# The first two outer sets of a masked-linear and gated-FFN kernel: multiplying x before or after its norm

## The chip, the cores and the metric

The kernel runs on one core of one Trainium2 chip. The metric is the device time of the core in microseconds (us): 513.37 is the median of three runs of the kernel before (513.25 to 513.42). TensorE multiplies; VectorE, ScalarE and GpSimd do elementwise work; SyncE's queue (SP) issues nearly all transfers between device memory and the on-chip memory. TensorE writes into eight accumulator banks, which VectorE and ScalarE can read[...].

## The reference, cut to what matters

x has 2048 rows (tokens) of 512 elements.

```python
xn  = (x - mean(x)) / sqrt(var(x) + eps)                 # per row
s   = xn @ (weight * block_mask).T                       # 512 x 512
nx  = xn * rsqrt(mean(xn * xn) + eps) * ln_w
h   = silu(nx @ gate_w.T) * (nx @ up_w.T)                # 1792 wide each
out = x + s * silu(h @ down_w.T)
```

## The kernel before, in words

**Layout.** Everything is kept transposed: features lie on the 128 partitions, tokens along the free axis, in tiles of 128 x 512 float32. The 2048 tokens are four tiles t; x^T has four feature chunks c. The norm and the RMS norm are joined in two factors per token, `scl` and `nb` (minus the mean times `scl`); a normalised x is `scl * x + nb`. `ln_w` is multiplied into the gate and up weights (`scaled`, `scale_a`).

**Products.** Each matrix product is done as Strassen-Winograd's seven products in place of eight, in two levels: an outer level over quarters of the matrices, and within it an inner level over quarters of these. The gate and up weights come as seven groups of 256 rows (g = 0 to 6), the masked weight is an eighth. For each group the outer level has seven sets q = 1 to 7. One set is one `instance`: seven products m = 1 to 7 of a 128 x 128 weight tile with a 128 x 512 tile of x^T. They are summed in accumulator banks named x, y and z with the set's number j: `x_2` is the bank x of set j = 2. An instance ends with four result tiles. Sets q = 1 and 2 of all groups come first (j = 0 to 15; q = 1 and 2 of group 0 are j = 0 and 1), because they use only the plain quarters; the results of q = 2 are q = 1's plus its own products (the `prior` of `instance`). Then come q = 6, 5, 7, 3 and 4, and last the down projection.

**Sums around the products.** The products m = 5, 6, 7 and 4 need differences of x^T tiles (`inner_b`, on VectorE and GpSimd), and m = 3, 5, 6 and 7 need sums of weight tiles (`inner_a`, four of them for q = 1 and 2 of a group, s1, s2, s4 and s3, on GpSimd). Between the products a bank is copied ("snap") or added to others ("seed", "total"), on ScalarE where there is no prior and on VectorE where there is.

**The start.** Sixteen 128-row blocks of x are loaded (`load_x`), each tile's statistics are taken on VectorE (`stats`), the factors are worked out (`factors`, with a square root on ScalarE), the blocks are scaled and shifted (`normalise`), transposed by TensorE into a bank (`transpose`) and copied out by ScalarE (`evacuate`). Only tiles 0 and 1 are needed by sets q = 1 and 2. Until the first transposes, TensorE does products of the identity with itself (`warm`).

**The order of the work.** It is written out by hand. `at(pos, fn)` files every step under a position, and at the end all steps are issued in the order of their positions. One position is the time of one product, and set j begins at 7j; `EARLY` and the positions T(us) set the start apart. So the order within each engine's queue is fixed. What must wait for what is settled by semaphores that the framework adds. Buffers are fixed slots of one array `mem` (rings with names such as B5, B7, acc), and banks rotate under four names (X 3, Y 2, Z 1, V 2). The transposes of tile 3, about positions 51 to 59, go into the V banks, as does `gate`, the result of the SiLU.

**After a set.** When group g's sets q = 1 and 2 are complete, `silu` (ScalarE) and `h_out` (VectorE's product of the gate, L414 before, L487 after) make the quarter of h from its four tiles, a column n at a time: n = 0 and n = 1. Set q = 1's four results go to `acc_dram[g]` and come back later for q = 6.

Of the kernel before, what the change touches and what calls it, by code (L numbers as in the profile page):

```python
# [8 lines left out]
F32 = mybir.dt.float32  # L9
# [22 lines left out]
def tile_masked_linear_gated_ffn(  # L32
# [19 lines left out]
    h_dram = tc.dram_tile([7, G, 2, P, W], F32, name="h_dram")  # L52
    s_dram = tc.dram_tile([KC, NTT, P, W], F32, name="s_dram")
    rms_dram = tc.dram_tile([NT], F32, name="rms_dram")
    acc_dram = tc.dram_tile([G + 1, P, 4, W], F32, name="acc_dram")
    dw_dram = tc.dram_tile([4, P, G, 256], F32, name="dw_dram")

# [25 lines left out]
    def slot(tag, name=None):  # L83
        i, n = ring[tag]
        ring[tag][0] += 1
        return mem[:, first_slot[tag] + i % n, :]
# [6 lines left out]
    def bank(tag, name):  # L93
        return ps.tile([P, W], F32, tag=tag, name=name, bufs=PSB[tag])
# [8 lines left out]
    ident = const.tile([P, P], F32, tag="ident", name="ident")  # L103
    blockones = const.tile([P, P], F32, tag="blockones", name="blockones")
    keep = const.tile([P, 4, 16], F32, tag="keep", name="keep")

    def constants():
        make_identity(nc, ident)
        nc.gpsimd.memset(blockones, 0.0)
        for b in range(P // BLK):  # L110
            nc.gpsimd.memset(blockones[b * BLK : (b + 1) * BLK, b * BLK : (b + 1) * BLK], 1.0)


    xt, raw, stat = {}, {}, {}
    agg = small.tile([P, NTT, TT, 2], F32, tag="agg", name="agg", bufs=1)
    rms = small.tile([P, NTT, TT], F32, tag="rms", name="rms", bufs=1)

    def load_x(t):
        for i in range(TT):
            xt[t, i] = mem[:, first_slot[("B6", "vc", "v5", "B4")[t]] + i, :]  # L120
            nc.sync.dma_start(xt[t, i], x[(t * TT + i) * P : (t * TT + i + 1) * P, :])

    def stats(t, i):
# [4 lines left out]
    def factors(t):  # L128


        scl = small.tile([P, TT], F32, tag="scl", name=f"scl_{t}")
        nb = small.tile([P, TT], F32, tag="nb", name=f"nb_{t}")
        stat[t] = (scl, nb)

        def last():
            nc.vector.reciprocal(scl, scl)
            nc.vector.scalar_tensor_tensor(nb, agg[:, t, :, 0], -1.0, scl, ALU.mult, ALU.mult)

        return [lambda: nc.vector.tensor_scalar(scl, agg[:, t, :, 1], 1.0 + EPS, EPS * EPS, ALU.mult, ALU.add),
                lambda: nc.scalar.activation(scl, scl, AF.Sqrt), last]  # L140

    def normalise(t, i, eng, cols=slice(0, W)):
        scl, nb = stat[t]
        v = xt[t, i][:, cols]
        if eng is dve:
            nc.vector.tensor_scalar(v, v, scl[:, i : i + 1], nb[:, i : i + 1], ALU.mult, ALU.add)
            return
        nc.scalar.activation(v, v, AF.Identity, bias=nb[:, i : i + 1], scale=scl[:, i : i + 1])

# [162 lines left out]
    def inner_a(g, part, k0=0, n=2):  # L312
# [8 lines left out]
        for k in range(n):  # L321
# [2 lines left out]
        return [lambda: add(pool, s1, a21, a22), lambda: add(pool, s2, s1, a11, ALU.subtract),  # L324
                lambda: add(pool, s4, a12, s2, ALU.subtract), lambda: add(pool, s3, a11, a21, ALU.subtract)]

    def weights(g, q, m):
        if q < 3 and m in (1, 2, 4):
            return aq[g, 0, q - 1][:, {1: 0, 2: 2, 4: 3}[m] * P :][:, :P]
        return aop[g, q][m]  # L330


    def instance(j, g, q, prior, dest, after):
# [1 line left out]

        st = {}

        seeded = j > 1

        def mm(m, tag, key, first):  # L340
            if first and key not in st:
                st[key] = bank("Y" if key == "z" and j == 1 else tag, f"{key}_{j}")
            nc.tensor.matmul(st[key], weights(g, q, m), operand(q, m), start=first and not (key == "z" and seeded),  # L343
                             stop=True, skip_group_check=True)

        def seed():

            if seeded:
                st["z"] = bank("Z", f"z_{j}")
                nc.scalar.copy(st["z"], st["x"])  # L350
            else:
                st["s1"] = slot("s2" if j else "s5", f"s1_{j}")
                if prior is None:
                    nc.scalar.copy(st["s1"], st["x"])
                else:
                    add(dve, st["s1"], st["x"], prior(0))
# [15 lines left out]
            else:  # L372
                add(dve, dest(i), st[key], prior(i))

        at(EARLY.get((j, 0), 7 * j + 1), seed)
        for off, m, tag, first, snapshot, out in (
            (0, 1, "X", True, None, None),
            (2, 5, "Y", True, ("s5", 3), None),
            (3, 2, "Z", True, None, (None, 0)),
            (4, 6, "X", False, ("s2", 1), None),  # L380
            (6, 3, "Y", False, None, ("s2", 1)),
            (8, 7, "X", False, None, ("s5", 3)),
            (12, 4, "X", False, None, (None, 2)),
        ):
            key, pos = tag.lower(), 7 * j + off
            at(EARLY.get((j, m), pos), mm, m, tag, key, first)
            if snapshot:
                at(pos + 1, snap, key, *snapshot)
            elif out:

                pos += 2.3 if prior is None and m == 2 and seeded else 1
                if m == 2:
                    pos = EARLY.get((j, "z"), pos)
                at(pos, total, key, *out)
                after(out[1], pos)


    def group(g, where):
# [39 lines left out]
        def summed(dst, src, into, then=None, engines=(pool,) * 4):  # L438
# [14 lines left out]
            3: (vc, vc, done(0, 1, vc)),  # L453
            4: (acc, acc, done(1, 0, acc)),
        }
        for q in setup:
            instance(where[g, q], g, q, *setup[q])

        def h_sum(q, n, tile_of, a, b):

# [2 lines left out]
            nc.sync.dma_start(h_dram[HD[q], g, n], o)  # L463

        sums, rest = slots(F["acc"] + 4 * (g % 2), 4), 7 * where[g, BLOCKS[0]]
        at(7 * where[g, 1] + 15, lambda: nc.sync.dma_start(acc_dram[g], sums))
        at(rest - (14 if g else 6), lambda: nc.sync.dma_start(sums, acc_dram[g]))
        if g < G:
            def again():
# [114 lines left out]
    def down_instance(o, q, where_, prior, dest, after):  # L584
# [78 lines left out]
        if last_set:  # L663
            at(where_(17) + 0.1, base_of_last)
            for part, pos in zip(parts, (where_(23), where_(24), where_(25))):
# [8 lines left out]
    where = {gq: j for j, gq in enumerate(order)}  # L674
    N = len(order)
    END = 7 * N
    T = lambda us: (us - 14.0) / 0.86
    EARLY.update({(0, 1): T(10.4), (0, 2): T(11.3), (1, 1): T(12.1), (1, 2): T(13.0), (0, 0): T(11.5), (1, 0): 4.3,
                  (0, "z"): 3.26, (1, "z"): 4.9})
    SILU = 26.2  # L680
    at(T(-10), constants)
    at(T(-10), load_x, 0)
    at(T(-10), lambda: nc.scalar.dma_start(lnw_sb, ln_w))

    at(T(-10), lambda: nc.gpsimd.tensor_copy(mem[:, F["a1"], 0:1], xt[0, 0][:, 0:1]))
    for K in range(2):
        at(T(-10), load_a, 0, K)
    at(T(-10), load_x, 1)
    for K in range(2):
        at(T(-10), load_a, 1, K)  # L690
    at(T(-10), load_x, 2)
    for K in range(2):
        at(T(-10), load_a, 2, K)
# [7 lines left out]
        for _ in range(n):  # L701
            nc.tensor.matmul(b[:, :P], ident, ident, start=True, stop=True, skip_group_check=True)

    at(T(1.4), lambda: warm(26, bank("V", "idle")))
    for t, p, step in ((0, T(7.1), 0), (1, T(12.5), 0), (2, 36.0, 1.2), (3, 36.1, 1.2)):
        plan(p, step, factors(t))
    for i in range(TT):
        half = act if i < 2 else dve
        at(T(3.7 + 0.82 * i), stats, 0, i)
        at(T(9.35 + 0.82 * i), stats, 1, i)  # L710
        for h, cols in enumerate((slice(0, W // 2), slice(W // 2, W))):
            at(T(7.95 + 0.9 * h + 0.4 * (i % 2)), normalise, 0, i, half, cols)
            at(T(13.45 + 0.9 * h + 0.4 * (i % 2)), normalise, 1, i, half, cols)
        for c in range(KC):
            at(T((8.9, 9.3, 9.8, 11.0)[c] + 0.05 * i), transpose, 0, c, (2, 3, 0, 1)[i], "XYYX"[c])
            at(T((14.35, 14.8, 15.25, 16.2)[c] + 0.05 * i), transpose, 1, c, (2, 3, 0, 1)[i], "XVVV"[c])
    at(T(6.0), scale_a, 0, 0, pool)
    at(T(6.1), scale_a, 0, 1, pool)
    for c in range(KC):
        at(T((9.75, 10.3, 10.85, 12.05)[c]), evacuate, 0, c, act)  # L720
        at((5.6, T(15.6), 6.0, 3.14)[c], evacuate, 1, c, act)
    for pos, q, m, eng in ((1.1, 1, 5, dve), (1.87, 1, 6, dve), (2.56, 1, 7, dve), (3.95, 2, 5, dve), (2.7, 1, 4, pool),
                           (4.6, 2, 6, dve), (7.2, 2, 7, dve), (5.0, 2, 4, pool)):
        at(pos, inner_b, q, m, eng)
    for q in (1, 2):
        for k in (0, 1):
            for n in (0, 1):
                at(8, outer_b, q, k, n, None)
    at(2.1, scale_a, 1, 0)
    at(5.2, scale_a, 1, 1)  # L730
    for i in range(TT):
        at(14.0 + 2.5 * i, stats, 2, i)
        at(25.0 + 3 * i, stats, 3, i)
        at((44.0, 51.0, 55.2, 58.2)[i], normalise, 2, i, act)
        at(40.5 + 2.4 * i, normalise, 3, i, dve)
    plan(36.2, 1.2, rms_factor())

    for t, p0 in ((3, 51.5), (2, 65.5)):
        n = t % 2
# [21 lines left out]
    for g in range(G + 1):  # L761
        p, rest = 7 * where[g, 1], 7 * where[g, BLOCKS[0]]
        for K in range(2):
# [3 lines left out]
                at(p - (10.4, 7.3)[K], lambda K=K: mask_a(aq[G, 0, K], 0, K))  # L767
            elif g > 1:
                at(p - (10.4, 7.3)[K], scale_a, g, K)
        if g:  # L770
            plan(p - 7, 1, inner_a(g, 1))
        else:
            plan(T(9.9), 0, inner_a(0, 1, 0, 1))
            plan(T(11.9), 0, inner_a(0, 1, 1, 1))
        at(rest - 29, load_block, g)

        def block_sums(g=g):
# [147 lines left out]
```

## Time and profile before

| | |
|---|---|
| median of three runs | 513.37 us |
| the profiled execution | 513.17 us |
| its span, from the first to the last instruction | 511.4 us |
| TensorE (PE) busy | 505.8 us, 99% |
| VectorE (DVE) busy | 380.4 us, 74% |
| GpSimd (POOL) busy | 340.9 us, 67% |
| ScalarE (ACT) busy | 182.6 us, 36% |
| transfers | 121.59 MB, mean 238 GB/s |

The busy shares are means over the whole span. "L702" is line 702 of the kernel that was run, and a line can be a helper's: L97 is every elementwise add. PEld is TensorE's loading of weights. A float32 product shows as two MATMUL records and two LDWEIGHTS records, a transpose as one of each. The span's parts are given in us from its start. In a table by windows the columns are the length, then for PE, PEld, DVE, ACT and POOL the busy us with the number of instructions, then the granted TensorE clock, the share of the transfer engines and GB/s. In a timeline they are the start, the time and the instruction, and in brackets how long the engine stood idle before it and what released it. A row by form has busy us and the mean ns of one, then the idle time before.

### The profile page before, as it was taken

The page shows a single profiled execution, that of the slowest core. Times are in us where ns is not written, and L with a number is a line of the kernel's source. Part 1 is how long each engine was busy: PE and PEld are TensorE (multiplying, and loading weights), DVE is VectorE, ACT ScalarE, POOL GpSimd, SP SyncE. Part 2 cuts the span into 40 slices and gives each one's busy share as a digit, 9 for nine tenths or more (in the row PEclk, how much of TensorE's full clock was granted, in tenths as well). Part 3 has the DMA queues.
Part 4 walks back from the last instruction along what each step waited for, and adds up shares of the span by engine and source line. Part 5 has one row for each costly group of instructions (what it writes and reads, how often), then busy time and mean ns, then how long its engine had stood idle before and what let it go on. Part 6 is the DMA issues. An engine that isn't in the chain of part 4 may idle for free. (4 is left out here: it accounts for less than half of the span.)

```text
span 511.4 us, 4943 instructions
## 1 busy us (share of the span) xinstructions
PE 505.8 (99%) x1269; PEld 231.8 (45%) x1269; DVE 380.4 (74%) x590; ACT 182.6 (36%) x348; POOL 340.9 (67%) x283
## 2 busy tenths in 40 slices
PE   8999999999999999999999999999999999999997
PEld 8444444444444444444444444444444444444444
DVE  6878689876977969699696978968747645367736
ACT  4656754633536353353634433330100101001111
POOL 5522224994795968869597789976662754739960
PEclk9999999999999999999999999999999999999999
DMA  8436636369159386785948667499997698476472
GB/s 289 164 132 238 247 133 227 135 236 350 48 219 348 147 302 228 238 289 208 338 166 294 209 239 254 169 332 383 357 339 270 204 374 327 146 252 216 151 229 83
DMA packets 60460, 121.59 MB, mean 238 GB/s; under 512 B 5760, under 2 KB 13328, under 8 KB 58384
## 3 DMA queue, kind: packets, MB, share of 16 engines
q1 hardware_dynamic: 60288, 121.27, 66.8%
q8 instruction: 10, 0.16, 0.1%
q14 instruction: 18, 0.15, 0.1%
q10 hardware_dynamic: 144, 0.00, 0.0%
HBM read 75.11 MB, written 46.15 MB: 237 GB/s over the span
## 5 line engine op out<-in xcount | busy, mean ns | idle before, releaser
L97 POOL TENSOR_TENSOR mem<-mem 128x512 f32<-128x512 f32 (+4 forms) x245 | 305.2, 1267 | 135.4 <-ACT mem L264 36.5
L343 PE MATMUL x<-mem 128*128 128x512 f32 x448 | 213.6, 595 | 0.2 <-DVE mem L97 0.2
L343 PEld LDWEIGHTS x<-mem 128*128 128x128 f32 x448 | 83.7, 190 | 107.3 <-issue 86.9
L97 DVE TENSOR_TENSOR mem<-x,mem 128x512 f32<-128x512 f32 x137 | 92.5, 684 | 42.0 <-PE x L343 41.1
L343 PE MATMUL y<-mem 128*128 128x512 f32 x224 | 114.5, 593 | 0.3 <-DVE mem L97 0.3
L97 DVE TENSOR_TENSOR mem<-mem 128x512 f32<-128x512 f32 (+3 forms) x60 | 74.7, 1252 | 7.8 <-PE dx L591 4.3
L591 PE MATMUL dx<-mem 128*128 128x512 f32 x174 | 78.3, 592 | 0.0
L97 DVE TENSOR_TENSOR mem<-y,mem 128x512 f32<-128x512 f32 x96 | 65.6, 684 | 9.8 <-PE y L343 8.5
L343 PEld LDWEIGHTS y<-mem 128*128 128x128 f32 x224 | 42.2, 190 | 53.0 <-issue 47.8
L350 ACT COPY z<-x 128x512 f32<-128x512 f32 x54 | 30.9, 573 | 97.9 <-PE x L343 92.2
L343 PE MATMUL z<-mem 128*128 128x512 f32 x112 | 57.3, 593 | 0.0
L591 PEld LDWEIGHTS dx<-mem 128*128 128x128 f32 x174 | 33.1, 190 | 41.6 <-issue 40.4
L591 PE MATMUL dy<-mem 128*128 128x512 f32 x98 | 44.5, 592 | 0.0
L409 ACT ACTIVATE gate<-mem 128x512 f32<-128x512 f32 x56 | 33.1, 601 | 25.3 <-DVE mem L97 20.9
L414 DVE TENSOR_TENSOR mem<-gate,mem 128x512 f32<-128x512 f32 x56 | 38.0, 681 | 5.1 <-POOL mem L97 4.3
L564 POOL TENSOR_TENSOR mem<-mem 128x512 f32<-128x512 f32 x16 | 25.0, 1570 | 15.3 <-DMA mem<-s_dram 15.2
L343 PEld LDWEIGHTS z<-mem 128*128 128x128 f32 x112 | 21.0, 190 | 24.9 <-issue 23.9
L574 ACT ACTIVATE silu<-mem 128x512 f32<-128x512 f32 x15 | 9.0, 602 | 64.6 <-DVE mem L97 48.3
L97 DVE TENSOR_TENSOR mem<-z,mem 128x512 f32<-128x512 f32 x41 | 28.0, 682 | 3.5 <-PE z L343 3.5
L591 PEld LDWEIGHTS dy<-mem 128*128 128x128 f32 x98 | 18.6, 190 | 23.4 <-issue 23.4
L97 DVE TENSOR_TENSOR mem<-dx,mem 128x512 f32<-128x512 f32 x16 | 11.0, 690 | 20.1 <-PE dx L591 20.1
L591 PE MATMUL dz<-mem 128*128 128x512 f32 x56 | 25.2, 592 | 0.0
(73 smaller groups left out, 289.2 us busy)
## 6 DMA issues: line engine op xcount, KB each, us to landing
h_dram<-mem SPq DMA_DIRECT2D x98, 256.0 KB, 2.1
mem<-h_dram SPq DMA_DIRECT2D x28, 768.0 KB, 6.2
mem<-in_gu SPq DMA_DIRECT2D x42, 256.0 KB, 3.7
acc_dram<-mem SPq DMA_DIRECT2D x8, 1024.0 KB, 4.2
mem<-acc_dram SPq DMA_DIRECT2D x8, 1024.0 KB, 6.7
mem<-in_x SPq DMA_DIRECT2D x16, 256.0 KB, 5.2
s_dram<-mem SPq DMA_DIRECT2D x16, 256.0 KB, 4.8
mem<-s_dram SPq DMA_DIRECT2D x16, 256.0 KB, 6.3
```

The source lines that it names most:

```text
L97: eng.tensor_tensor(o, a, b, op)
L343: nc.tensor.matmul(st[key], weights(g, q, m), operand(q, m), start=first and not (key == "z" and seeded), stop=True, skip_group_check=True)
L350: nc.scalar.copy(st["z"], st["x"])
L409: nc.scalar.activation(gate[key], t(), AF.Silu)
L414: nc.vector.tensor_mul(a(), gate[key], b())
L564: at_later.append(lambda: nc.gpsimd.tensor_tensor(s_tile, s_tile, rms_bc[t], ALU.mult))
L574: nc.scalar.activation(b[0][:, part], y[:, part] if source is None else source(), AF.Silu)
L591: nc.tensor.matmul(st[key], w(), b(), start=first and key != "z", stop=True, skip_group_check=True)
```

## The change

Sets j = 0 and 1 (group 0, q = 1 and 2) no longer use the normalised and transposed x. The kernel loads the eight tiles of x^T that they need straight from an input that holds x transposed (`raw_x`), takes the differences from them (`raw_t`) and multiplies these. The norm is made good afterwards: for a weight row w, w (scl x + nb) is scl (w x) + nb sum(w).

- The row sums of group 0's weights are TensorE products with a column of ones (`sum_rows`, eight products of one column).
- The factors `scl` and `nb` of tiles 0 and 1 lie token by token on the partitions. They are transposed by TensorE, copied by ScalarE, stored in device memory and read back as four tiles with the same row on all partitions (`fac_store`).
- Each of the eight results is multiplied by the row of `scl` on GpSimd and a shift is added there; the shift is ScalarE's product of the row of `nb` with the row sum. Then q = 1's and q = 2's tiles are added (`raw_results`): for each of the four tile places i, five GpSimd operations. The two sets have no prior any more, and their results lie in other slots. `acc_dram[0]` is stored at position 49.
- Normalising, transposing and evacuating tiles 0 and 1 move behind the products of j = 0 and 1, for use from j = 2 on, and parts of the normalising go to GpSimd. The scaling of group 0's first weights moves from GpSimd to ScalarE, that of group 1's from ScalarE to GpSimd.
- The loads' order changes: group 0's weights and the eight x^T tiles come ahead of x. The one-column GpSimd copy that kept the weights behind the first block of x is gone. The idle products are 8 and no longer 26.
- `EARLY` and the positions of the start are written anew, with 9.9 in the place of 14.0 in T.

The diff, cut to its core:

```diff
+    def raw_x(q, k, n, eng=nc.sync):
+        o = rop[q, k, n] = mem[:, RQ[q - 1][2 * k + n], :]
+        c = 2 * (q - 1) + k
+        eng.dma_start(o, x_t[c * P : (c + 1) * P, n * W : (n + 1) * W])
...
+    def sum_rows(rs, K):
+        for r in range(2):
+            for c in range(2):
+                nc.tensor.matmul(rs[:, 2 * K + r : 2 * K + r + 1], aq[0, 0, K][:, (2 * c + r) * P :][:, :P], ones,
+                                 start=c == 0, stop=c == 1, skip_group_check=True)
+
+    def fac_store():
+        b = bank("V", "fac_rows")
+        nc.tensor.transpose(b[: 4 * TT, :P], fac.rearrange("p a t i -> p (a t i)"), ident)
+        rows = small.tile([4 * TT, P], F32, tag="fac_rows", name="fac_rows", bufs=1)
+        nc.scalar.copy(rows, b[: 4 * TT, :P])
+        nc.sync.dma_start(fac_dram.rearrange("a t (i p) -> (a t i) p", p=P), rows)
+        for a in range(2):
+            for t in range(2):
+                nc.sync.dma_start(fac_bc(a, t), fac_dram[a, t].unsqueeze(0).to_broadcast([P, W]))
...
+    def raw_results(p1, c11, silu, h_out):
+
+        tmp = [mem[:, F["B7"] + k, :] for k in range(7)] + [mem[:, F["B5"] + 1, :]]
+
+        def shift(K, i):
+            r, n = divmod(i, 2)
+            nc.scalar.mul(tmp[4 * K + i], fac_bc(1, n), row_sums[:, K, r : r + 1])
+
+        pos = 22.0
+        for n in (0, 1):
+            for i in (n, n + 2):
+                at(pos - 0.1, shift, 0, i)
+                at(pos, lambda i=i, n=n: add(pool, p1(i), p1(i), fac_bc(0, n), ALU.mult))
+                at(pos + 1.5, lambda i=i: add(pool, p1(i), p1(i), tmp[i]))
+                at(pos + 2.9, shift, 1, i)
+                at(pos + 3, lambda i=i, n=n: add(pool, c11(i), c11(i), fac_bc(0, n), ALU.mult))
+                at(pos + 4.5, lambda i=i: add(pool, c11(i), c11(i), tmp[4 + i]))
+                at(pos + 6, lambda i=i: add(pool, c11(i), c11(i), p1(i)))
+                pos += 7.5
+            at(pos + 0.2, *silu(n))
+            at(pos + 1.5, *h_out(n))
...
-        at(7 * where[g, 1] + 15, lambda: nc.sync.dma_start(acc_dram[g], sums))
+        if g:
+            at(7 * where[g, 1] + 15, lambda: nc.sync.dma_start(acc_dram[g], sums))
+        else:
+            at(49, lambda: nc.sync.dma_start(acc_dram[0], slots(R1, 4)))
...
-    T = lambda us: (us - 14.0) / 0.86
+    T = lambda us: (us - 9.9) / 0.86
...
     at(T(-10), constants)
+    at(T(-10), load_a, 0, 0)
+    at(T(-10), lambda: nc.scalar.dma_start(lnw_sb, ln_w))
+    at(T(-10), raw_x, 1, 0, 0, nc.scalar)
...
-    at(T(-10), lambda: nc.gpsimd.tensor_copy(mem[:, F["a1"], 0:1], xt[0, 0][:, 0:1]))
...
-    at(T(1.4), lambda: warm(26, bank("V", "idle")))
+    at(T(1.4), lambda: warm(8, bank("V", "idle")))
+
+    at(T(4.0), scale_a, 0, 0)
+    at(T(6.3), scale_a, 0, 1)
...
+    at(T(17.0), row_sums_of, 0)
+    at(T(21.2), row_sums_of, 1)
+    at(T(22.4), fac_store)
```

## The prediction

> **What bounds the kernel now.** I read the page's busy shares first, then the windows of the stages, then the engines' timelines of the first 75 us. From the page:
>
> ```profile
> PE 505.8 (99%) x1269; PEld 231.8 (45%) x1269; DVE 380.4 (74%) x590; ACT 182.6 (36%) x348; POOL 340.9 (67%) x283
> ```
>
> TensorE leaves 5.6 us of 511.4 idle, so only its useless work can be saved. Windows (columns: length, then busy us of PE, PEld, DVE, ACT, POOL):
>
> ```profile
> 18.00:24.00 6.00, 5.66 (x17) 2.21 (x16) 5.90 (x11) 3.46 (x7) 4.14 (x5) 1.00 0.02 8
> 24.00:30.00 6.00, 6.00 (x16) 2.81 (x15) 4.22 (x9) 2.87 (x6) 1.14 (x2) 1.00 0.62 221
> 30.00:40.00 10.00, 10.00 (x25) 4.41 (x24) 8.87 (x17) 6.36 (x12) 2.87 (x4) 1.00 0.30 106
> 40.00:60.00 20.00, 20.00 (x51) 8.98 (x50) 15.91 (x35) 15.10 (x29) 5.67 (x8) 1.00 0.60 221
> 60.00:100.00 40.00, 40.00 (x117) 19.25 (x116) 34.39 (x54) 23.13 (x45) 19.22 (x19) 1.00 0.51 186
> ```
>
> From 24 us PE has no idle time: whatever is lost later cannot be won back. The rest is the start, TensorE's timeline:
>
> ```profile
> 1.35 8.98 PE L702 MATMUL idle<-ident 128*128 128x128 f32 x52 [1.35 <-POOL ident masks.py:199]
> 10.16 1.47 PE L155 MATMUL pt<-ident,mem 128*128 128x128 f32 x12
> ...
> 62.06 0.60 PE L155 MATMUL pt<-ident,mem 128*128 128x128 f32 x4
> ```
>
> Real work starts at 10.16; before it run 26 idle products. A real product (two records) comes each 0.86 us, four transposes take 0.44. The line at 62.06 is `pt_3_0`, my later mark. The idle products alone, in windows:
>
> ```profile
> 6.35:7.35 1.00, 1.00 (x7) 1.00 (x6) 1.00 1.05 393
> 7.35:8.35 1.00, 1.00 (x10) 1.00 (x10) 1.00 0.80 248
> ```
>
> TensorE is slow until about 7.4 us, though the granted clock says 1.00 throughout. ScalarE's and GpSimd's timelines:
>
> ```profile
> 0.72 0.41 ACTq L683 DMA_DIRECT2D lnw_sb<-in_ln_w  x1
> 1.16 1.28 ACT L140 ACT_TABLE_LOAD   x1 [1.16 <-PEq L912]
> 7.09 0.21 ACT L140 ACTIVATE scl<-scl 128x4 f32<-128x4 f32 x1 [4.64 <-DVE scl L139]
> ...
> 31.63 3.02 POOL L97 TENSOR_TENSOR mem<-mem 128x256 f32<-128x256 f32 x4 [6.49 <-ACT mem L264]
> 44.10 1.54 POOL L97 TENSOR_TENSOR mem<-mem 128x256 f32<-128x256 f32 x2 [9.46 <-ACT mem L264]
> ```
>
> One table load, and it waits for nothing. GpSimd has large gaps up to 60 us, but its weight sums (`inner_a`) wait for ScalarE's scaled weights. Forms of GpSimd up to 60 us:
>
> ```profile
> L97 POOL TENSOR_TENSOR mem<-mem 128x256 f32<-128x256 f32 x16 | 11.5, 728 | 26.5 <-ACT mem L264 15.9 <-PE x L343 9.9
> L97 POOL TENSOR_TENSOR mem<-mem 128x512 f32<-128x512 f32 x2 | 2.6, 1279 | 4.6 <-DVE mem L97 4.6
> ```
>
> **What the Trainium skill says.** "TensorE: Matmul & The Clock Gate", Part 1: the array runs at half clock until a free-running window of about 3.4 us has been busy; the two windows above agree (7 and 10 records per us). The same page, architectural detail (engine queue depths): "ACT/DVE are strict FIFO", so a waiting instruction holds all behind it; the chain below rests on it. "ScalarE: Activation LUTs", What ACT_TABLE_LOAD costs: about 1283 ns; the trace has 1.28 us. "GPSIMD Engine Reference", section 3: a two-input elementwise operation takes about twice VectorE's time; here 1.28 against 0.64 to 0.68.
>
> **The change, part by part, in time of the trace.** The instruction order of the built kernel (no times in it) gives waits and neighbours.
>
> *Loads.* Removed: GpSimd's copy that held the first weight load until x landed. Added ahead of x: eight x_t tiles, 256 KB each, seven on SP's queue and one on ScalarE's. At some 380 GB/s each takes 0.69 us, so x lands 5.5 us later (10.3 to 12.3, not 3.6 to about 6). Hidden: x is not needed before the products below are done.
>
> *First product.* Its weights are now scaled by ScalarE, and the table load in front now carries the wait for `ln_w`, issued at 0.72, 3.0 to land: 3.72 + 1.28 + 0.50 (half a weight tile, L264's mean) = 5.5. The eight idle products end at about 4.1. Bounds: 4.5 if the table load did not wait, 6.5 if loads crowd.
>
> *Products of sets 0 and 1.* Thirteen in a row, 13 x 0.86 = 11.2. A half-clock 512-wide product isn't in the trace; by the page twice 0.86. I take two of them (a busy window of 3.4 us after 5.5); none to four is possible: +1.7 (0 to 3.4). End 18.45. GpSimd's eight 128-wide sums (0.46 each) and VectorE's differences keep ahead.
>
> *A bubble.* The square root now needs a second table load, since the first holds another set; it stands behind the copy of `x_1` after its product m = 6 (ready at 17.0, copy 0.58). Then 1.28, root 0.21, VectorE's reciprocal and shift 0.45, three half tiles by ScalarE at 0.52: 21.2. TensorE waits 2.7.
>
> *To the second tile's norm.* 16 transposes 1.8, 0.3 of waiting for an evacuation, five products 4.3, the factor transpose 0.15 and eight one-column products. Those have no row; 16 records at the idle products' later 0.1 us make 1.6 (0 if hidden, 2.7 at the slow rate). End 29.4. ScalarE's copy of the row sums stands ahead of its normalising, which so begins at 29.7; half tiles 1.05, transposes 0.9, first difference 0.65: `y_2`'s first product runs at 32.15, against 26.84 before.
>
> *To GpSimd's start.* `x_2`'s product m = 6 ends at 34.6; ScalarE copies it (35.3 with what is queued), evacuates three tiles (1.7), scales the second half of group 2's weights (0.9): 37.95. GpSimd's s1 and s2 (2 x 0.75) end at 39.45. The factor rows (one 8 KB store; four broadcasts of 256 KB, all on SP's queue) leave at 31.5; with 2 to 4 to land and then 3 to 4 they arrive by 36 to 39.5, just hidden. Group 3's weights queue behind them, landing by 41, needed at 45.
>
> *The added 20 operations on GpSimd.* Five for each of four row-and-column tiles, 20 x 1.27 = 25.4, with eight `inner_a` sums of groups 2 to 4 between them in the queue, 8 x 0.75 = 6.0: 31.4, all in order, ended at 70.85. A multiply may be cheaper (GpSimd's mask multiply has mean 1045 ns): down to 29.6. The eight shifts on ScalarE (each some 0.7, 5.6 in all) lie beside it, in a stage where it was busy 15.1 of 20 us.
>
> *Who waits.* VectorE's product of the gate (L487, group 0, second column) waits for GpSimd's last sum: 70.85 + 0.7 = 71.6. It holds the bank that `pt_3_0` needs, and it stands ahead of `x_7`'s copy. So TensorE starts `pt_3_0` at 71.6, against 62.06: **+9.6**. Already the first column (GpSimd done at 54.4) holds VectorE and with it the copy that `x_5`'s product m = 7 needs, which comes to about 58.4, against 50.0: +8.4. Without GpSimd the start alone has `x_4` begin at 40.6 against 37.15: +3.5; the queue takes that in.
>
> *Later stores.* `acc_dram[0]` (1 MB) goes out late, behind GpSimd on SP's queue; the next loads have tens of us. Nothing after `pt_3_0` gives time back.
>
> Sum: the profiled execution, 513.17, its span 511.4 and 1.8 around it, plus 9.6 = 522.8. The median of the runs is 513.37, 0.2 away, which doesn't matter here.
>
> **Rivals.** (1) The start alone: +3.5, 516.7. It holds if GpSimd is through with the first chain some 6 us sooner, by cheaper operations and an earlier start. Against it: 25.4 us of new work in one queue. (2) Faster: GpSimd's chain ends by 61.4, so that `pt_3_0` isn't held, and TensorE gains the idle products: start at 4.5, not 10.16 (-5.7), one-column and factor work +1.75, a bubble +0.9: -3.0, 510.2. It decides from a GpSimd start at 30.0. Against it: ahead of that start lie 20 products (17.2), 28 transposes (3.4) and the small ones (1.75), from 4.5 to 26.9, then ScalarE 3.6 and s1, s2 1.5: 32, even with no stall at all. (3) Worse: the long half-clock start, waits of TensorE that throttle it again, a shift late on a full ScalarE: +14, 527. That the products don't move to raw x is excluded: the built order shows them first.
>
> **How the numbers follow.** No change can be told from measurement below about 0.2% (1 us). GpSimd's chain decides: 0.58, 519 to 526 (start of the chain 36 to 43). Start alone, 514.4 to 519: 0.20. Worse: 0.12. Faster: 0.07. Within 0.2%: 0.03. The range 515.5 to 528.5 leaves out the faster and the equal case and tails of two others, about 0.2. So faster 0.07, same 0.03, slower 0.90.
>
> **What would show it.** First L393 product near 5.5, behind a table load that ends near 5; a table load near 17.5 and TensorE idle near 18 to 21; GpSimd without gaps from about 40 to 71; VectorE's L487 waiting for GpSimd twice, and TensorE idle for several us behind each. Wrong if GpSimd's chain begins before 33, if its operations take under 1.1 us, or if TensorE runs on while VectorE waits.

## The result

| | before | after |
|---|---|---|
| median of four runs each, side by side | 513.31 us | 529.13 us (528.17 to 529.70) |
| ratio, 95% interval | | 1.0307 (1.0289 to 1.0325) |
| the profiled execution, its span | 513.17, 511.4 us | 529.70, 527.7 us |

The changed kernel is slower by 15.8 us: 6.3 more than the 522.8 of the prediction, and just above its range. Its busy shares on the page, and the same five windows as in the prediction:

```profile
PE 509.1 (96%) x1250; PEld 229.2 (43%) x1250; DVE 385.4 (73%) x588; ACT 190.0 (36%) x362; POOL 372.4 (71%) x308
```

```profile
18.00:24.00 6.00, 4.41 (x13) 2.45 (x13) 4.25 (x11) 4.83 (x9) 5.54 (x9) 0.80 1.04 383
24.00:30.00 6.00, 5.76 (x24) 3.33 (x23) 1.82 (x7) 1.76 (x4) 0.47 (x1) 0.91 0.08 31
30.00:40.00 10.00, 8.88 (x39) 4.87 (x37) 7.48 (x14) 7.43 (x17) 2.71 (x3) 1.00 0.29 87
40.00:60.00 20.00, 15.58 (x35) 6.20 (x34) 15.62 (x34) 12.95 (x23) 19.53 (x20) 0.98 0.41 156
60.00:100.00 40.00, 36.77 (x104) 17.24 (x105) 34.37 (x54) 25.70 (x49) 17.06 (x18) 0.93 0.57 207
```

TensorE, which had no idle time from 24 us on, now lacks 4.4 us in 40 to 60 and 3.2 in 60 to 100; GpSimd is full from 40 to 60. The granted clock, 1.00 before in every window, is below it in four of the five. Rows of TensorE's timeline of after, others between them left out:

```profile
5.71 1.10 PE L393 MATMUL x<-mem 128*128 128x512 f32 x2 [0.79 <-DMA mem<-in_x_t]
20.65 0.87 PE L162 MATMUL pt<-ident,mem 128*128 128x128 f32 x3 [1.32 <-DVE mem L153]
42.75 1.88 PE L393 MATMUL x<-mem 128*128 128x512 f32 x4
62.67 2.07 PE L393 MATMUL x<-mem 128*128 128x512 f32 x2 [6.44 <-DVE mem L98]
64.53 1.75 PE L393 MATMUL y<-mem 128*128 128x512 f32 x2
76.58 1.02 PE L393 MATMUL y<-mem 128*128 128x512 f32 x2
77.66 0.66 PE L162 MATMUL pt<-ident,mem 128*128 128x128 f32 x4
```

The line at 42.75 is the first product of `x_4`, the one at 62.67 `x_5`'s product m = 7 behind a block of 6.44 us, the last `pt_3_0`. The line at 64.53 is a product at half clock: the next one starts 1.59 us later, not 0.86. `pt_3_0` shows no wait: the product ahead of it starts 1.08 us earlier, only 0.22 more than a product takes. At which times these marks, and the late product `pm` of the mask's sums, stood:

| mark, us | before | predicted | after | after less before |
|---|---|---|---|---|
| first real product | 10.16 (a transpose) | 5.5 | 5.71 | -4.45 |
| `x_4` begins | 37.15 | 40.6 | 42.75 | +5.60 |
| `x_5`, m = 7 | 50.02 | 58.4 | 62.67 | +12.65 |
| `pt_3_0` | 62.06 | 71.6 | 77.66 | +15.60 |
| `pm` | 85.29 | | 101.11 | +15.82 |
| span | 511.4 | 521.0 | 527.7 | +16.3 |

Nearly all of the loss is there by `pt_3_0`: 5.60 us at `x_4`, 7.05 more by `x_5`'s product, and only 2.95 behind that, of which 1.73 are two products at half clock. The rest of the document asks what made up the 15.8, and where the missing 6 came from. Rows of ScalarE's and GpSimd's timelines of after:

```profile
3.62 1.28 ACT L271 ACT_TABLE_LOAD   x1 [3.62 <-DMA mem<-in_gu]
18.11 1.28 ACT L147 ACT_TABLE_LOAD   x1
...
38.57 27.33 POOL L98 TENSOR_TENSOR mem<-mem 128x512 f32<-128x512 f32 x25 [2.51 <-DMA mem<-fac_dram]
68.90 2.70 POOL L98 TENSOR_TENSOR mem<-mem 128x512 f32<-128x512 f32 x2 [3.00 <-ACT mem L454]
73.01 5.25 POOL L98 TENSOR_TENSOR mem<-mem 128x256 f32<-128x256 f32 x6 [1.41 <-ACT mem L271]
```

The chain is there as described, but it has gaps of 3.00 us (a shift of ScalarE, L454, came late) and 1.41. And VectorE's timeline, from the gate's first column to the copy that releases `x_5`'s product, then the second column:

```profile
56.19 0.69 DVE L487 TENSOR_TENSOR mem<-gate,mem 128x512 f32<-128x512 f32 x1 [2.95 <-POOL mem L98]
...
58.19 0.77 DVE L146 TENSOR_SCALAR scl<-agg 128x4 f32<-128x4 f32 x2
58.88 0.70 DVE L178 TENSOR_SCALAR rms<-agg 128x16 f32<-128x16 f32 x1
59.62 0.25 DVE L179 RECIPROCAL rms<-rms 128x16 f32<-128x16 f32 x1
59.90 0.90 DVE L180 TENSOR_TENSOR rms<-agg,rms 128x16 f32<-128x16 f32 x1
60.84 1.18 DVE L181 TENSOR_SCALAR rms<-rms 128x16 f32<-128x16 f32 x1
61.93 0.68 DVE L98 TENSOR_TENSOR mem<-x,mem 128x512 f32<-128x512 f32 x1
...
76.91 0.69 DVE L487 TENSOR_TENSOR mem<-gate,mem 128x512 f32<-128x512 f32 x1 [1.59 <-POOL mem L98]
```

VectorE waits for GpSimd at both columns (2.95 and 1.59 us), as predicted. TensorE was held for long behind the first only. But operations of 16 elements a row, 0.16 to 0.34 us before, take 0.70, 0.90 and 1.18: from L487 to the copy it is 5.7 us, where the 4.0 us that the prediction has from GpSimd's last sum to the product leave 3.3.

### The profile page after: what moved, and what is told of

Read it like the earlier page. It is cut to its first block, busy times and chain, and to the rows that moved or that the text cites. A ratio compares the mean times of both kernels' runs of the same rounds, so it can differ in the third digit from the quotient of the medians.

```text
span 527.7 us, 4979 instructions
## 1 busy us (share of the span) xinstructions
PE 509.1 (96%) x1250; PEld 229.2 (43%) x1250; DVE 385.4 (73%) x588; ACT 190.0 (36%) x362; POOL 372.4 (71%) x308
## 5 line engine op out<-in xcount | busy, mean ns | idle before, releaser
L98 POOL TENSOR_TENSOR mem<-mem 128x512 f32<-128x512 f32 (+4 forms) x268 | 335.4, 1274 | 124.8 <-ACT mem L421 32.3
L393 PE MATMUL x<-mem 128*128 128x512 f32 x448 | 216.6, 600 | 8.4 <-DVE mem L98 7.4
L98 DVE TENSOR_TENSOR mem<-x,mem 128x512 f32<-128x512 f32 x135 | 91.0, 683 | 36.4 <-PE x L393 35.6
L98 DVE TENSOR_TENSOR mem<-mem 128x512 f32<-128x512 f32 (+3 forms) x65 | 78.7, 1219 | 17.1 <-DMA mem<-in_x_t 9.1
L487 DVE TENSOR_TENSOR mem<-gate,mem 128x512 f32<-128x512 f32 x56 | 38.2, 682 | 10.6 <-POOL mem L98 7.5
```

The lines of the kernel that those rows point to most:

```text
L98: eng.tensor_tensor(o, a, b, op)
L393: nc.tensor.matmul(st[key], weights(g, q, m), (raw_operand if j < 2 else operand)(q, m), start=first and not (key == "z" and seeded), stop ...
L487: nc.vector.tensor_mul(a(), gate[key], b())
```

## The experiments

Theory at first (the prediction's): a late start, carried into one queue on GpSimd, for whose results VectorE waits in order. The rivals that the trace of after raised: GpSimd slows VectorE's own work by running beside it; TensorE's half clock after each idle stretch; ScalarE's shifts.

**e1 and e5: without the 20 operations.** The same kernel twice: the norm of the two sets isn't made good.

```diff
-                at(pos - 0.1, shift, 0, i)
-                at(pos, lambda i=i, n=n: add(pool, p1(i), p1(i), fac_bc(0, n), ALU.mult))
... the other three GpSimd steps and the second shift too
```

> Leaves out the 20 GpSimd operations and the eight ScalarE shifts, so the eight results stay unscaled; all else as in the changed kernel. If GpSimd's chain and those who wait for it cost what the start does not (x_4 starts at 42.75 against 37.15, 5.6 late), the time is 513.3 + 5.6 + 0.7 = 519.6, pt_3_0 starts at about 67.7, and VectorE's L487 waits for nobody for long. If the start and its transfers are the whole cause, and the chain only fills time lost anyway, it stays within 2 us of 529. VectorE's small operations before the root (L178 to L181), which took up to 1.18 us beside GpSimd, go back to 0.16 to 0.35 if GpSimd's work slowed them.

One execution: 524.94 us, neither the 519.6 nor the 529 of the expectation. VectorE's small operations were back at 0.17 to 0.18 us and `x_5`'s product waited 0.77, but `x_4` began only at 46.03. Its windows (clock in the third column from the end), then those of e5:

```profile
22.00:30.00 8.00, 8.00 (x27) 4.92 (x25) 3.09 (x9) 2.06 (x5) 2.46 (x4) 0.57 0.32 118
36.00:40.00 4.00, 4.00 (x11) 2.06 (x12) 3.02 (x5) 2.05 (x6) 1.27 (x1) 0.59 0.53 153
```

```profile
22.00:30.00 8.00, 7.55 (x38) 4.66 (x36) 4.40 (x14) 3.05 (x8) 2.18 (x4) 1.00 0.29 109
36.00:40.00 4.00, 3.58 (x8) 1.05 (x6) 3.96 (x9) 1.75 (x5) 3.03 (x4) 1.00 0.81 272
```

> The same kernel as e1: the 20 GpSimd operations and the eight ScalarE shifts are left out, so sets q = 1 and 2 of group 0 keep their unscaled results. e1's one execution had TensorE at half clock in 22 to 30 and 36 to 40 us and began x_4 only at 46.0. If that was an accident of one execution, the median of several is 519.5 to 521.5 (the start of x_4 near 41 and nothing lost after it). If the moved start itself costs that much, the median stays at 524 to 525 and the later work costs only 4 to 5 us of the 15.8.

Median 519.96 (ratio 1.0137, 1.0121 to 1.0153), `x_4` at 40.99, `pt_3_0` at 66.93. So the moved start alone costs 6.75 us (519.96 less the 513.21 beside it): 4.87 by `pt_3_0`, the rest after it (0.6 more by `pm`, and some 1.0 behind TensorE's last products), whose causes weren't followed up. The five us between e1 and e5 are TensorE's clock alone, in one and the same program.

**e2: the gate out of the way.** The SiLU and L487 of group 0 work on other data, so that nothing on VectorE waits for GpSimd; the 20 operations and the shifts stay.

```diff
-            raw_results(tiles(R1), c1, lambda n: (silu, (0, 0, n), lambda: c1(n)),
+            raw_results(r1, c1, lambda n: (silu, (0, 0, n), lambda: mem[:, F["B6"] + n, :]),
... and other slots for q = 1's and q = 2's results
```

> Keeps all 20 GpSimd operations and all shifts. Only the SiLU and the gate's product of group 0 take other tiles (normalised x that lies there), and four tiles are moved so that no later step waits for the chain through its buffers; that part of h is not the true one. If the wait of VectorE behind GpSimd is what costs, the time is that of the kernel without the operations, about 519.6, though GpSimd works the same 25 us. If GpSimd's work itself costs (its weight sums late, its port shared with VectorE), the time stays near 525 to 529.

525.37 (one execution), far from 519.6. L487 no longer waited, and still `x_5`'s product did, for VectorE:

```profile
57.97 1.29 PE L393 MATMUL x<-mem 128*128 128x512 f32 x2 [3.34 <-DVE mem L98]
```

Ahead of it three of VectorE's small operations (L178, L180 and L181) took 0.48 to 1.18 us, without any wait for GpSimd. So of the 9.2 us that lie between e5 and after, 5.4 are still there when nothing waits for GpSimd's sums. That points to GpSimd's running, and not the wait for it, as the larger part. It doesn't show it: the shifts still run, some 1.7 us are half clock behind the wait above, and this is one execution.

**e10: a bystander.** The test of that: e5 with twenty additions on GpSimd into a scratch tile. Nobody waits for them, and there are no shifts.

```diff
+                for d in (0, 1.5, 3, 4.5, 6):
+                    at(pos + d, lambda: add(pool, tmp[4], tmp[5], tmp[6]))
```

> The same as e5 (the norm of the two sets is not made good, no ScalarE shifts), with twenty GpSimd additions of two 128 x 512 tiles into a scratch tile at the places of the removed ones; nothing waits for them. If GpSimd slows VectorE's small operations and so TensorE, these take 0.6 to 1.2 us again, x_5's product waits 2 to 4 us, and the total is 522 to 525 against e5's 519.96. If only the waits for GpSimd's results count, it stays at 520 within 0.6.

Median 526.20 (ratio 1.0275, 1.0221 to 1.0329; 524.70 to 531.31): 6.2 more than e5, for work that no instruction depends on. Some of VectorE's operations by form from 50 to 66 us, first of e5, then of e10:

```profile
L98 DVE TENSOR_TENSOR mem<-x,mem 128x512 f32<-128x512 f32 x6 | 4.1, 680 | 1.0 <-PE x L393 1.0
L153 DVE TENSOR_SCALAR mem<-mem,scl,nb 128x512 f32<-128x512 f32 x4 | 2.2, 541 | 0.0
L129 DVE BATCH_NORM_STATS2 st<-mem 128x6 f32<-128x512 f32 x1 | 0.7, 683 | 0.0
L144 DVE SCALAR_TENSOR_TENSOR nb<-agg,scl 128x4 f32<-128x4 f32 x2 | 0.3, 164 | 0.1
L178 DVE TENSOR_SCALAR rms<-agg 128x16 f32<-128x16 f32 x1 | 0.2, 165 | 0.0
```

```profile
L153 DVE TENSOR_SCALAR mem<-mem,scl,nb 128x512 f32<-128x512 f32 x4 | 4.9, 1218 | 0.0
L98 DVE TENSOR_TENSOR mem<-x,mem 128x512 f32<-128x512 f32 x4 | 2.7, 672 | 0.0
L144 DVE SCALAR_TENSOR_TENSOR nb<-agg,scl 128x4 f32<-128x4 f32 x2 | 1.7, 838 | 0.1
L129 DVE BATCH_NORM_STATS2 st<-mem 128x6 f32<-128x512 f32 x2 | 1.4, 684 | 0.0
L178 DVE TENSOR_SCALAR rms<-agg 128x16 f32<-128x16 f32 x1 | 1.2, 1241 | 0.0
```

`x_5`'s product waited 2.17 us, within the 2 to 4 expected. The median is above the 522 to 525 expected with it, and the executions differ: by the interval the 6.2 may be some 3 to 9, but the quickest of e10 is still 3.2 us above the slowest of e5 (521.48).

The slowing is selective. A sum with one operand in a bank (672 against 680 ns) and the statistics (684 against 683) are untouched; the scalings and the two-operand products out of on-chip memory go from 541 to 1218, 164 to 838 and 165 to 1241. It doesn't catch each one: L181, 1.18 us in after and in e2, took 0.17 here. This is what the Trainium skill says in "SBUF — State Buffer", Who interferes with whom: VectorE's second pair of ports is GpSimd's, a VectorE instruction in a two-port mode (scalings can enter one) or with two inputs from that memory needs it, and whichever comes second "fully blocks" for the whole instruction of the other. The additions of up to 1.1 us agree: GpSimd's instruction lasts 1.27. `pt_3_0` (70.64) stood 3.7 us behind e5's. Of these 0.7 were there at `x_4` (41.67 for 40.99), before the additions began, by first products at half speed in this execution, so 3.0 are the additions'. These could also have cost by keeping GpSimd's weight sums waiting in its queue, but from 38 to 75 us TensorE waited for GpSimd once, for 0.2 us, and VectorE and ScalarE not once. In the profiled execution some 4 more were lost behind `pt_3_0`, at a place that I hadn't in mind:

```profile
76.38 0.69 DVE L98 TENSOR_TENSOR mem<-pt,mem 128x512 f32<-128x512 f32 x1 [4.85 <-DMA h_dram<-mem]
```

```profile
78.32 1.33 PE L393 MATMUL x<-mem 128*128 128x512 f32 x2 [2.35 <-DVE mem L98]
79.64 2.04 PE L393 MATMUL y<-mem 128*128 128x512 f32 x2
```

A sum of VectorE waits for a store that had been issued late, TensorE 2.35 us for the sum, and then come products at half clock. In e5 the same wait of VectorE is 2.4 us long and TensorE doesn't feel it.

**e3: the shifts early.** Two of the shifts on ScalarE go ahead of the block, and group 4's weight sums on GpSimd 2.1 positions back.

```diff
-                at(pos - 0.1, shift, 0, i)
+                at(pos - 0.1 if i < 3 else 37.0, shift, 0, i)
-                at(pos + 2.9, shift, 1, i)
+                at(pos + 2.9 if i < 3 else 40.0, shift, 1, i)
-            plan(p - 7, 1, inner_a(g, 1))
+            plan(p - (4.9 if g == 4 else 7), 1, inner_a(g, 1))
```

> The last two shifts are put at positions 37 and 40 in ScalarE's queue, from 44.4 and 47.4, and group 4's weight sums behind the chain's last sum, from the middle of it. If the chain's two gaps (3.0 us behind a shift, 1.4 behind a weight scaling) and the sums between are what took pt_3_0 from the predicted 71.6 to 77.66, it starts near 72 and the time is 523 to 524. If GpSimd's own work set the end, no more than 1 us is gained.

529.43 (one execution), no gain. GpSimd had its gapless chain and `pt_3_0` came at 74.66, 3.0 earlier than in after (2.0 of it were there at `x_4`, which began at 40.79 in this execution). Nearly all of it was lost again, for the most part to the wait that e10 shows too:

```profile
36.61 32.85 POOL L98 TENSOR_TENSOR mem<-mem 128x512 f32<-128x512 f32 x29 [2.51 <-DVE mem L98]
...
80.20 0.69 DVE L98 TENSOR_TENSOR mem<-pt,mem 128x512 f32<-128x512 f32 x1 [4.65 <-DMA h_dram<-mem]
```

The trace shows more. The chain with all 20 operations ended at 69.46, before the 70.85 of the prediction, and still `pt_3_0` was no earlier than 74.66. In these two rows of TensorE's timeline the block at `x_5` was there as before; VectorE's product of the second column no longer waited for GpSimd, and no wait stands just ahead of `pt_3_0`; so that block, with the half clock behind it, held it, and not the second column.

```profile
60.75 2.08 PE L393 MATMUL x<-mem 128*128 128x512 f32 x2 [6.47 <-DVE mem L98]
74.66 0.60 PE L162 MATMUL pt<-ident,mem 128*128 128x128 f32 x4
```

In e2, e9, e11 and e12, where q = 1's last result lies in another slot, this wait is absent. That it was a matter of this slot wasn't tried alone.

**e6: the small operations behind the copy.** VectorE's factors of tiles 2 and 3 come 1.2 positions later.

```diff
-    for t, p, step in (... (2, 39.2, 1.2), (3, 39.3, 1.2)):
+    for t, p, step in (... (2, 40.4, 1.2), (3, 40.5, 1.2)):
... normalise of tile 3 and the RMS factor moved by as much
```

> Complete kernel after; the small VectorE operations of the factors of tiles 2 and 3 and of the RMS factor go from ahead of x_5's copy to behind it (1.2 positions later). Theory that GpSimd slows them (about 4 us in place of 1.2 ahead of the copy): x_5's product m = 7 comes at 59 to 60 us instead of 62.7, the block behind it is shorter, but the second product of the gate still waits for GpSimd's chain, so the total falls only by 1 to 3, to 526 to 528. Rival, that only the wait for GpSimd counts: x_5's product stays at 62 to 63 and the total at 528.5 to 529.5.

Median 528.68 (ratio 1.0316, 1.0274 to 1.0357). `x_5`'s product came at 58.77, 3.9 us earlier, and the shift that had been late was in time (GpSimd's gap 0.25 for 3.00). The total gained nothing, and so lies where the expectation put it for the case that the small operations don't matter; but `x_5`'s product moved as the theory said, and the second column no longer waited. TensorE was held elsewhere instead (rows of its timeline):

```profile
58.77 1.90 PE L393 MATMUL x<-mem 128*128 128x512 f32 x2 [2.71 <-DVE mem L98]
66.70 1.12 PE L393 MATMUL x<-mem 128*128 128x512 f32 x2 [2.05 <-DVE mem L98]
72.42 0.33 PE L162 MATMUL pt<-ident,mem 128*128 128x128 f32 x1 [0.83 <-DVE mem L153]
```

The traces of after and e6 together show a loop in after: the wait for GpSimd holds VectorE, with it the small operations whose root ScalarE waits for in order, behind that a shift, and for this GpSimd waits in turn.

**e4, e7 and e8: the start.** e4 loads the root's table first, by a root of one column at the beginning. e7 puts twelve idle products into TensorE's idle time ahead of the transposes. e8 has e4's edit, and puts both row sums into that idle time, with ScalarE's copy of them earlier.

```diff
+    at(T(-10), lambda: nc.scalar.activation(junk, ones, AF.Sqrt))     # e4, e8
+        warm(12, pt[0, 0])                                            # e7, at T(16.3)
-    at(T(17.0), row_sums_of, 0)                                       # e8
-    at(T(21.2), row_sums_of, 1)
+    at(T(16.3), row_sums_of, 0)
+    at(T(16.3), row_sums_of, 1)
+    at(T(17.8), copy_sums)
```

> A square root of a column of ones, whose result nobody uses, is put ahead of all on ScalarE, so the root's table is loaded once, early, and waits for no transfer. If the second table load is on the path, the bubble before the first transposes shrinks from some 2.4 us by 1.3, perhaps with the half clock after it (1.4 us), and GpSimd's chain starts 1.3 to 2.7 us sooner: 526.5 to 528. If the statistics or x's landing end the bubble anyway, no change: 529.

> Complete kernel after, with twelve idle products of the identity (about 0.1 us a record, 2.4 us in all) on TensorE ahead of the first transposes, where it stood idle for 1.3 to 2.7 us. Theory that this idle time makes TensorE run at half clock for some us afterwards: the granted clock stays near 1.0 from 18 to 30 us, x_4 begins at 40.5 to 41.5 instead of 42.75, and the total falls by 1 to 2, to 527 to 528. Rival, that the half clock has another cause: products of 1.9 us after the bubble as before, and 529 to 530.

> Complete kernel after, with the start mended: the root's table is loaded first (as in e4), both row sums stand in TensorE's idle time ahead of the first transposes, and ScalarE's copy of them comes earlier. If the late start carries on to the end through GpSimd's chain: x_4 begins at 37.5 to 39 (42.75), the chain starts 3 to 5 us earlier and the total is 524 to 525.5. If the chain is bound by something else (the factor rows in device memory, ScalarE's shifts), it starts no sooner than 40 and the total stays at 527 to 529.

e4: 526.99 (one execution), transposes at 19.51 for 20.65, `x_4` at 39.88; since this execution had no half clock there, not all of the 2.1 us are the table's. e7: 530.15 (ratio 1.0325, 1.0308 to 1.0342), above the 529 that was expected for no gain. The clock did stay at 1.00 until 32.2, but then, after idle spells of 0.63 and 0.44 us among transposes, the half clock came there:

```profile
30.40 1.37 PE L162 MATMUL pt<-ident,mem 128*128 128x128 f32 x8 [0.63 <-ACT mem L155]
32.20 2.04 PE L393 MATMUL y<-mem 128*128 128x512 f32 x2 [0.44 <-DVE mem L98]
```

My account of the half clock, that this one idle stretch causes it, fell. e8: 524.76 (ratio 1.0226, 1.0209 to 1.0243). `x_4` began at 37.76, at full clock from 18 us on, and everything behind it stood 5.0 us earlier than in after, the block as long as there (rows of TensorE's timeline):

```profile
57.68 2.07 PE L393 MATMUL x<-mem 128*128 128x512 f32 x2 [6.44 <-DVE mem L98]
72.67 0.66 PE L162 MATMUL pt<-ident,mem 128*128 128x128 f32 x4
```

So of the 5.0 us gained ahead of the chain, 4.4 reached the end.

**e9, e11 and e12: less work ahead of the gate.** On e8's start, the results of both sets are added while GpSimd is idle, and only the sum is scaled and shifted before the gate: eight operations in the chain for twenty. The eight on q = 1's own results follow at positions 52 to 66. The computation is complete.

```diff
+            at(pos, lambda i=i: add(pool, c11(i), c11(i), p1(i)))      # early, unscaled
...
+                at(pos, lambda i=i, n=n: add(pool, c11(i), c11(i), fac_bc(0, n), ALU.mult))
+                at(pos + 1.5, lambda i=i: add(pool, c11(i), c11(i), soon[i]))
... e11: gate at positions 38 and 45.4, factors of tiles 2 and 3 at 46.8
... e12: these factors at 44.2, and ten idle products
```

> Complete computation, on the start of e8. The results of sets q = 1 and 2 are added before they are scaled (four GpSimd additions in its idle time near 24 to 30 us, the row sums added too), so that only eight of the operations stand ahead of the gate (four a column, 5.1 us each with the shifts beside it) and not ten a column; the eight operations on q = 1's own results come at positions 52 to 66, when nothing waits for them. If GpSimd's length ahead of the gate is what costs the rest, x_5's product m = 7 waits less than 1 us, the chain ends near 47 and the total is 513.5 to 515.5. If GpSimd's load on VectorE costs as much wherever it stands, 516 to 519.

520.47 (ratio 1.0151, 1.0134 to 1.0168): both halves of the expectation missed. The gate stood too early, and VectorE waited for GpSimd:

```profile
44.11 0.69 DVE L493 TENSOR_TENSOR mem<-gate,mem 128x512 f32<-128x512 f32 x1 [3.30 <-POOL mem L98]
```

> Complete computation; e9 with three things moved so that nothing waits for GpSimd and little of VectorE's small work runs beside it: the two columns of the gate stand at positions 38 and 45.4 (28.2 and 34.2 in e9, where VectorE waited 3.3 us), two of the early additions stand behind the products' differences on GpSimd (in e9 they slowed the second tile's factors), and the small operations of the factors of tiles 2 and 3 follow the second column. If waits and slowed small operations are all that is left, x_4 begins near 37.8, TensorE waits under 1 us from there to 80, and the total is 514 to 516. If the added work itself costs more (ScalarE's shifts, VectorE's larger operations beside GpSimd), 517 to 520.

517.82 (ratio 1.0098, 1.0080 to 1.0116). The small operations were at 0.17 us again and nothing waited for GpSimd; the largest wait left was 1.5 us of TensorE for tile 3's scalings, bunched too late by my move. The total lies in the expectation's second range (517 to 520), by another cause than the one that it names.

> Complete computation; e11 with the small operations of the factors of tiles 2 and 3 and the normalising of tile 3 some two positions earlier (in e11 the transposes of tile 3 waited 1.5 us for them), the second column of the gate behind them, the root of the second tile's factors ahead of two evacuations, and ten idle products at the start instead of eight, so that TensorE's idle time before the first product is shorter. The waits of e11 (1.5 us at 59 to 61) go: 514.5 to 516. If the ten idle products also end the half clock of the first two or three products: 512.5 to 514, the only way in which it comes out level with the kernel before. If ScalarE's root now holds its evacuations, 517 or more.

518.85 (516.94 to 519.91; ratio 1.0116, 1.0101 to 1.0131), not better than e11. In the profiled execution, the quickest, the first products ran at full clock and `x_4` began at 37.53, but a copy of ScalarE held TensorE for 1.97 us. No version that I ran beats the kernel before; e11, the best, is still 4.7 us behind.

## Why the prediction was right and wrong

The direction, the two products of the gate that wait for GpSimd, and the idea that nothing after `pt_3_0` gives time back were right. What failed is the step *Who waits*: it has `pt_3_0` released at 71.6 by the second product of the gate, behind GpSimd's last sum. TensorE was held elsewhere, once and for 6.44 us, at `x_5`'s product behind the first column, where VectorE's small operations ran beside GpSimd at up to seven times their time; and behind the second column, where the +9.6 was placed, it hardly waited. e3 shows that the second column didn't set the time: the chain ended 1.4 us before the predicted end, and `pt_3_0` stood 3.1 us behind the predicted time.

The 6.06 us by which `pt_3_0` was off (77.66 for 71.6) lie along TensorE's path as follows: 1.7 by the first column's later start, 2.6 from there to `x_5`'s product, and 1.8 from that product to `pt_3_0` (14.99 us for 13.2), about what the two products at half clock behind the wait cost (1.73). That half clock follows such waits is in the third rival, but not in the sum. Step by step:

- *Loads* and *first product*: x was hidden, and the first product came at 5.71 for 5.5. Its last wait was for a tile of x^T, though, and not for the scaled weights.
- *Products of sets 0 and 1*: the end was 19.3 for 18.45. The two half-clock products weren't there in after, but small waits were, of 0.92 us for x^T's difference among others. In e10's profiled execution the products of the start were slow, three of them 1.59 to 1.83 us apart. A product at half clock takes 1.70 us (22.81 to 24.51 in after), so twice 0.86 was the right size.
- *A bubble*: transposes at 20.65 for 21.2, behind the second table load as described. That the time is so near is in part luck: the products ended 0.9 us later than predicted, and the last wait was 1.32 us and not 2.7. e4 gave it a value: the transposes came 1.1 us earlier with the table loaded first.
- *To the second tile's norm*: `y_2` at 33.98 for 32.15. I priced half clock at the first products, and not behind the bubble. The clock of 0.50 from 22 to 24 us made up most of it: e5, with the same start at full clock, had `x_4` at 40.99, against 40.6 predicted and 42.75 in after.
- *The added 20 operations on GpSimd*: the work was priced right, 31.1 us for 31.4. "All in order, ended at 70.85" failed: it ended near 76.9, 1.9 of this by the later start and 4.4 by the gaps. This end didn't set `pt_3_0`, as e3 shows. Behind the larger gap stands the sentence that the shifts "lie beside it": they lay in ScalarE's queue behind operations that wait for VectorE.
- *Who waits*: the first column came at 56.1 for 54.4; from there `x_5`'s product took 6.6 us for 4.0. The term that was missing is VectorE's small operations beside GpSimd, which I had at their unloaded times: 2.4 us ahead of this one copy.

The prediction's sums hold but for roundings of up to 0.15 us (its terms up to `y_2` give 32.3, for 32.15), which play no part here.

The third rival (527) named two things that the trace of after shows, TensorE throttled again after waits, and a late shift on ScalarE; taking the late shift away (e3) gained nothing. None of the rivals had GpSimd slowing VectorE, though the Trainium skill's "GPSIMD Engine Reference", whose section 3 gave me a price, has it in section 1, Specifications: the interfaces to on-chip memory are shared with VectorE. I took from it what an operation costs, and not what two engines share.

What the 15.8 us are made of, by medians: 6.75 the moved start (e5), 6.2 GpSimd's running beside VectorE, with what follows from it (e10 less e5, some 3 to 9), and 2.9 the remainder, in which the waits for its results and the shifts must lie. This remainder isn't clear of noise: the interval of after (1.0289 to 1.0325) lies within that of e10 (1.0221 to 1.0329). The last two parts aren't independent either: e2 without the waits has one execution at 525.37, e3 and e6 each take away one of the waits and gain nothing, because the next one stands close behind. Of the start's part 4.4 us were undone where it was mended (e8), of the chain's some, by shortening and moving it (e9, e11). How much of the second part is half clock and how much the late store isn't separated; one run of e10 took 525.06, 5.1 more than e5's median, at a mean granted clock of 1.00.

## What to carry to other kernels

Work moved to an idle engine isn't free because the engine is idle: ask which ports it shares, list the operations of its neighbour that use them, and price these at their blocked time, up to the length of the other's instruction. Where a wait is removed and nothing is gained, look for the next one a few us behind: here the wait for the gate, the slowed factors and a late store took one another's place. Time lost ahead of such a chain passed to the end for the most part (4.4 of 5.0 us in e8), so the start is worth mending too.

## What the runs showed of the hardware

- GpSimd's additions of 1.27 us slowed VectorE's scaling of 128 x 512 from 541 to 1218 ns and one of 128 x 16 from 165 to 1241 ns, and left a sum with a bank operand at 672 to 680 ns. The effect is by form, not by size, and doesn't catch each operation (L181 of 128 x 16 took 1.18 us in after and 0.17 in e10).
- TensorE fell to half clock after idle spells of no more than 1.32 us in a row, with transposes and one-column products around them. The clock then was 0.50 for some 3 us (22.0 to 25.0 in after), at a place that differed between executions of one program: e1 and e5 lie 5 us apart by it. The Trainium skill, "TensorE: Matmul & The Clock Gate", What's actually happening, calls the window free-running, which fits. Its condition is an idle window of some 3.4 us. None of these idle spells is as long, but the stretch without a 512-wide product is 3.5 us in after (19.3 to 22.8) and 3.3 in e7 (28.9 to 32.2); in e5 a stretch of 3.3 us passed at full clock. Whether transposes and one-column products count as idle wasn't tried. In e10 a wait of 2.35 us between two 512-wide products was enough (clock 0.50 from 80 to 82 us).
- The granted clock doesn't show each slow product: in e10 the first three start 1.59 to 1.83 us apart from 5.83 on, at a granted clock of 1.00.
- The one-column float32 products took 0.81 us for each four (eight records, from 22.99 to the next product's start at 23.80 in e7), 0.10 us a record, so 1.6 in all at full clock, as worked out from the idle products.
